# A scan over channel states: GpSimd's products made for two slots at once instead of one

## The chip, the cores and the metric

The kernel runs on one core of a Trainium2 chip. A core has five engines with queues of their own: TensorE (PE in the profile; its weight loads are PEld), VectorE (DVE), ScalarE (ACT), GpSimd (POOL) and SyncE (SP), which here issues all the transfers. Each engine works through its instructions strictly in the order in which the program lists them, and waits at an instruction until semaphores tell that its inputs are there and its output buffer is free. The metric is the device time of one execution in microseconds (us).

## The reference

The input x is 8 samples of 512 channels of 48 x 48 points (2304 points in a row, called L). Two layers are added to it in turn:

```python
x = x + L0_conv_ref(_gn(x), Wq, bq, Wkv, bkv)        # causal linear attention, 8 heads of 64
x = x + L1_conv_ref(_gn(x), in_proj_w, conv_w, ...)  # four blocks of a state-space scan
```

`_gn` is a group norm. The first layer projects to q, k and v, takes elu + 1 of q and k, and sums k v over the points before each point. The second takes the 512 channels as four blocks of 128; a block adds the result of the block before and runs this on its 256 inner channels d and 16 states n:

```python
dA = exp(delta[b,l,d] * A[d,n]);  dBu = delta * xs * Bm[b,l,n]
h = dA_t * h + dBu_t                     # over l, for each d and n
y = sum over n of h * C_t                # then + xs * D, times silu(z), projected to 128
```

so each sample has four blocks one after another, and each block 256 x 16 recurrences of 2304 steps.

## The kernel before, in words

The points are cut into 6 chunks of 384 (`LC`). One chunk of one block of one sample is a *job*; there are 8 x 4 x 6 = 192. A job is cut into 8 *slots* (`SLOTS`): slots 0 to 3 for the first half of the inner channels, 4 to 7 for the second, each slot four recurrences of 128 partitions (two values of `NG`, two groups of channels). The 128 partitions hold 64 channels by two states, so that one job needs 8 x 4 scans. There are 1536 slots and 6144 scans. Two *streams* (samples of even and of odd number) take turns, so that one can prepare while the other scans.

The work of slot k:

- `last_product` (L856, GpSimd): B times delta*xs for the last 128 of the 384 columns (`TAIL`), of both groups and both values of `NG`: 512 elements a partition. It takes the tile `u`, of which there are 5; ScalarE copies the state left by the chunk before into column 0 (L855).
- `product` (L867, VectorE): the same for the first 256 columns, 1024 elements. One input, `dxp`, lies in PSUM, copied there by ScalarE in `inputs` (L840).
- `decay` (L877, ScalarE): exp(delta A) into a PSUM bank, one for each scan, up to three ahead. Six banks are shared with attention's and the preparation's matmuls.
- `scan` (L888, VectorE): four times, over 385 columns in place in `u`.
- `weigh` (GpSimd): copies the last column to `state` (L902, in all but the last chunk) and multiplies `u` by C (L904), 1536 elements a partition.
- `gather` (L911, TensorE): eight matmuls that sum over the states into `yp`. After slots 3 and 7 `gated` (L923, VectorE) multiplies `yp` by silu(z), and `skip` (L845, ScalarE) begins `yp` anew with xs*D.

The order is written out by hand in `slot(k)`: product of slot k+1; in slots 2 and 6 the gated product; tasks that are due (`beside`); the scans; after the second scan the sums of slot k-2, the small product of slot k+2 and again tasks; at the end `weigh` of slot k. A half of a slot is the unit of time in which tasks are due. Tasks are generators that yield at each step the half in which the next one is due, and how many PSUM banks it needs:

- `prepare` of a job, begun 21 halves before its first slot: the convolution and the gate (L693, L704), softplus, delta written to DRAM (`dscr`, L773), then multiplied by xs in place on GpSimd (L805, two products), written again (`xscr`), and all read back spread over the partitions: `dr`, `dxr` (L784) and the rows of B and C (`rows`, L797: for each of four quarters one tile of B and one of C, two transfers of 192 KB each, 4 tiles of each kind).
- `chunk`: attention for one of the four head pairs o and one chunk c; 192 of them, placed by `times` (L293 projects with `wq_sb`, which holds all projections of q, k and v in SBUF, 3 MB). Where o is 0, GpSimd normalises the input first (L317, four pieces).
- `pass_on`: the hand-over from block to block; on GpSimd fu (L662), xi (L667) and xo (L670) for each chunk.
- `statistics` of a sample and `weights` of a block (L539 on GpSimd, four products).

All transfers stand in SP's one queue in the order of these steps; a transfer whose buffer isn't free yet holds up those behind it.

Of the kernel before, what the change touches and what calls it, by code (L numbers as in the profile page):

```python
# [9 lines left out]
F32 = mybir.dt.float32  # L10
# [7 lines left out]
P = 128  # L18
# [32 lines left out]
def attention_then_mamba_kernel(  # L51
# [50 lines left out]
    wq_sb = cpool.tile([P, 4, 1536], F32, name="wq_sb")  # L102
# [3 lines left out]
    def load_projections(o):  # L106

        src = wqkv.rearrange("(t p) c -> p t c", p=P)
        for j in range(3):
            cols = slice(j * 512 + o * P, j * 512 + (o + 1) * P)  # L110
            nc.sync.dma_start(out=wq_sb[:, :, cols], in_=src[:, :, cols])
# [104 lines left out]
    def statistics(b):  # L216
# [3 lines left out]
        if b == 0:  # L220

            xs = []

            def load(c):
                t = mpool.tile([P, 4, 1 + LC], F32, tag="u", name=f"xs_{c}", bufs=5)[:, :, 0:LC]
                nc.sync.dma_start(out=t, in_=xv[:, :, c * LC : (c + 1) * LC])
                xs.append(t)

            for c in range(5):
                load(c)  # L230
            load_projections(0)
            for c in range(NC):
                for ct in range(4):
                    nc.vector.bn_stats(stats[:, ct, c, :], xs[c][:, ct, :])
                if c == 0:
                    load(5)
                    fetch(0)
            for o in range(1, 4):
                load_projections(o)
# [33 lines left out]
    def chunk(m):  # L273
# [16 lines left out]
        def project(j):  # L290
            ps = bank()[:, 0:LC]
            for kt in range(4):
                nc.tensor.matmul(  # L293
                    ps,
                    wq_sb[:, kt, j * 512 + o * P : j * 512 + (o + 1) * P],
# [44 lines left out]
        fetch(m + 1)  # L340
        if o:
# [156 lines left out]
    class Stream:  # L498
# [62 lines left out]
        def pass_on(self):  # L561
# [52 lines left out]
            if last and self.z:  # L614

                got = [
                    mpool.tile([P, 4, 1 + LC], F32, tag="u", name=f"end_{i}", bufs=5)
                    for i in range(NC // 2)
                ]
                for c in range(NC):  # L620
# [53 lines left out]
    class Job:  # L674
# [6 lines left out]
        def prepare(self):  # L681
# [98 lines left out]
            src = scr.rearrange("(q i m f) l -> q m i (f l)", q=4, m=2, i=2)  # L780
# [13 lines left out]
            def rows(m, q):  # L794
                t = mpool.tile([P, NG, LC], F32, tag="BC"[m], name=f"{'BC'[m]}_{n}_{q}", bufs=4)
# [20 lines left out]
            rows(0, 1)  # L816
            self.prepared = True
            yield first - 3, 0
            rows(0, 2)
            yield first - 2, 0  # L820
            rows(1, 0)
            yield first - 1, 0
            rows(0, 3)
            yield first, 0
            rows(1, 1)
# [3 lines left out]
            rows(1, 2)  # L829
            yield first + 3, 0  # L830
            steps(1)
            yield first + 4, 0
            rows(1, 3)

        prepared = closed = False

# [12 lines left out]
        def last_product(self, s):  # L849

            shape, cols = [P, NG, 2, TAIL], slice(LC - TAIL, LC)
            u = mpool.tile([P, NG, 2, 1 + LC], F32, tag="u", name=f"u_{self.n}_{s}", bufs=5)
            if self.c:
                h, q = s // 4, s % 4 * NG
                nc.scalar.copy(u[:, :, :, 0], self.state[:, h, q : q + NG, :])  # L855
# [403 lines left out]
```

## Time and profile before

| what | value |
|---|---|
| runs | 8785.19, 8786.02 and 8791.31 us, median 8786.02 |
| profiled execution, first to last instruction | 8790.1 us, 4.1 over the median |
| first scan, last scan begin at | 229.4 and 8767.3 us |
| busy: VectorE, GpSimd, TensorE, ScalarE | 8067.0, 8044.8, 7766.8, 6744.5 us |
| 6144 scans on VectorE | 5457.0 us, mean 0.939 |
| 1536 products by C on GpSimd | 4882.7 us, mean 3.179 |
| 1536 small products on GpSimd | 1960.9 us, mean 1.277 |
| transfers | 1642.98 MB, 16 engines 69% busy |
| granted TensorE clock, mean | 0.964 |

The profile's own execution spans 8790.1 us; its time on the device is not listed apart from that. "Busy" is the union of an engine's instructions; a product's mean is somewhat longer than the time from its start to the next one's, since neighbours overlap by a few hundredths. A line of the waits says who waited, for whom, the total, how often, and the longest. A line of groups says line, engine, operation, tiles, shapes and count, then the busy time, the mean in ns, and the idle time just before with what ended it. Partitions come first in a shape: 128x1536 is 1536 elements on each of 128 partitions.

### The profile page before, as it was taken

The numbers are of one execution on the slowest core, as the hardware profiler recorded it, in microseconds if no ns is written. First come the engines' busy times: TensorE is split into PE (matmuls) and PEld (weight loads), VectorE is DVE, ScalarE is ACT, GpSimd is POOL, SyncE is SP. The second block draws the span as 40 slices with busy tenths as digits, with TensorE's granted clock in tenths as the row PEclk, the third lists the DMA queues.
The fourth block names the chain that finished last, engine by engine and source line by source line (L and its number), as shares of the span: only waits on it lengthen the run. The fifth ranks groups of instructions, "written<-read, shape, count | busy, mean of one in ns | idle before, by whom it ended". The sixth has DMA issues, their size and how long they took to land.

```text
span 8790.1 us, 122627 instructions
## 1 busy us (share of the span) xinstructions
PE 7766.8 (88%) x36482; PEld 3705.4 (42%) x36482; DVE 8067.0 (92%) x11078; ACT 6744.5 (77%) x13220; POOL 8044.8 (92%) x5623
## 2 busy tenths in 40 slices
PE   7899999998899899998889999999888999999865
PEld 4444444444444444444444444444444444444422
DVE  2899999999899999998889999999889999999998
ACT  2777887777788878777778878877777888877875
POOL 1789999999999999999999999999999999999998
PEclk9999999999999999999999999999999999999977
DMA  5667777766676777776667677777667666766655
GB/s 184 166 174 189 193 197 195 190 188 186 190 191 188 191 195 198 196 190 189 179 190 192 188 191 198 198 195 188 188 183 191 189 187 187 189 187 185 183 156 144
DMA packets 1002907, 1642.98 MB, mean 187 GB/s; under 512 B 138592, under 2 KB 797312, under 8 KB 1002240
## 3 DMA queue, kind: packets, MB, share of 16 engines
q1 hardware_dynamic: 1002240, 1635.13, 69.0%
q8 instruction: 291, 4.77, 0.2%
q14 instruction: 376, 3.08, 0.1%
HBM read 1309.06 MB, written 325.58 MB: 186 GB/s over the span
## 4 chain that ended last, share of the span: by engine, by line
DVE 28%; POOL 20%; ACT 14%; DMA 13%; PE 13%; issue 7%; SPq 4%; POOLq 0%; DVEq 0%; ACTq 0%
DVE u L888 19%; POOL u L904 11%; ACT bank L877 5%; DVE u L867 5%; POOL u L856 4%; PE bank L693 4%; PE bank L293 3%; PE yp L911 3%; DMA C<-scr 3%; SPq L797 2%; DMA dscr<-delta 2%; ACT L877 2%; DMA B<-scr 1%; ACT L764 1%; POOL delta L805 1%
## 5 line engine op out<-in xcount | busy, mean ns | idle before, releaser
L888 DVE TENSOR_TENSOR_SCAN u<-bank,u 128x385 f32<-128x385 f32 (+1 forms) x6144 | 5457.0, 939 | 350.1 <-ACT bank L877 300.3
L904 POOL TENSOR_TENSOR u<-u,C 128x1536 f32<-128x1536 f32 x1536 | 4882.7, 3179 | 121.9 <-DVE gm_m L182 16.9
L877 ACT ACTIVATE bank<-dr,av 128x385 f32<-128x385 f32 (+1 forms) x6144 | 3413.6, 578 | 752.3 <-DVE u L888 611.9
L911 PE MATMUL yp<-u,cst 128*64 128x384 f32 x12288 | 2440.7, 519 | 428.2 <-POOL u L904 355.9
L856 POOL TENSOR_TENSOR u<-B,dxr 128x512 f32<-128x512 f32 x1536 | 1960.9, 1277 | 16.5 <-DMA dxr<-xscr 13.8
L867 DVE TENSOR_TENSOR u<-B,dxp 128x1024 f32<-128x1024 f32 x1536 | 1836.0, 1195 | 11.3 <-ACT dxp L840 11.1
L293 PE MATMUL bank<-xn,wq_sb 128*128 128x384 f32 x4608 | 1680.1, 508 | 82.2 <-POOL xn L317 40.1
L911 PEld LDWEIGHTS yp<-u,cst 128*64 128x64 f32 x12288 | 782.0, 140 | 1660.6 <-issue 842.6
L693 PE MATMUL bank<-xi,wk 128*128 128x384 f32 x3072 | 1117.8, 507 | 218.5 <-ACT kl L390 112.5
L293 PEld LDWEIGHTS bank<-xn,wq_sb 128*128 128x128 f32 x4608 | 849.0, 195 | 826.5 <-DVE u L888 119.6
L693 PEld LDWEIGHTS bank<-xi,wk 128*128 128x128 f32 x3072 | 560.6, 192 | 780.8 <-ACT kl L390 202.1
L805 POOL TENSOR_TENSOR delta<-delta,xs 128x384 f32<-128x384 f32 x384 | 384.4, 1001 | 278.0 <-DMA dscr<-delta 215.9
L305 ACT ACTIVATE ex<-bank,bqkv_sb 128x384 f32<-128x384 f32 x384 | 221.0, 576 | 523.8 <-PE bank L293 523.6
L877 ACT ACT_TABLE_LOAD x382 | 490.1, 1283 | 6.7
L845 ACT ACTIVATE yp<-xs,pv 128x384 f32<-128x384 f32 x384 | 223.8, 583 | 290.8 <-DVE yz L923 289.3
L902 POOL COPY state<-u 128x4 f32<-128x4 f32 x1280 | 242.4, 189 | 172.6 <-DVE u L888 170.0
L753 PE MATMUL bank<-dbc,wd 9*128 9x384 f32 x768 | 315.6, 532 | 1.2 <-ACT dbc L745 1.1
L929 PE MATMUL bank<-yz,wo 128*128 128x384 f32 x768 | 299.2, 506 | 18.5 <-DVE yz L923 14.6
L704 PE MATMUL bank<-xi,wi 128*128 128x384 f32 x768 | 285.9, 494 | 10.9 <-ACT xs L729 10.9
L740 PE MATMUL bank<-xs,wx 128*40 128x384 f32 x768 | 281.0, 489 | 2.6 <-ACT sm L457 2.6
L923 DVE TENSOR_TENSOR yz<-yp,sz 128x384 f32<-128x384 f32 x384 | 211.6, 551 | 62.5 <-PE yp L911 62.3
L423 PE MATMUL bank<-cst,rdb 128*128 128x128 f32 x576 | 113.0, 311 | 170.7 <-DVE u L888 168.5
(117 smaller groups left out, 8018.7 us busy)
## 6 DMA issues: line engine op xcount, KB each, us to landing
B<-scr SPq DMA_DIRECT2D x1536, 192.0 KB
C<-scr SPq DMA_DIRECT2D x1536, 192.0 KB
xn<-xn SPq DMA_DIRECT2D x192, 768.0 KB
dr<-dscr SPq DMA_DIRECT2D x768, 192.0 KB
dxr<-xscr SPq DMA_DIRECT2D x768, 192.0 KB
dscr<-delta SPq DMA_DIRECT2D x192, 384.0 KB
xscr<-delta SPq DMA_DIRECT2D x192, 384.0 KB
xn<-in_x SPq DMA_DIRECT2D x48, 768.0 KB
```

The lines of the kernel that those rows point to most:

```text
L293: nc.tensor.matmul(ps, wq_sb[:, kt, j * 512 + o * P : j * 512 + (o + 1) * P], xn[:, kt, :], start=(kt == 0), stop=(kt == 3),)
L693: nc.tensor.matmul(xc, wk[:, k, h * P : (h + 1) * P], xi[:, c0 + k : c0 + k + LC], start=(k == 0), stop=(k == 3),)
L704: nc.tensor.matmul(zp, wi[:, 256 + h * P : 256 + (h + 1) * P], xi[:, c0 + 3 : c0 + 3 + LC], start=True, stop=True,)
L753: nc.tensor.matmul(vp, wd[32:41, h * P : (h + 1) * P], dbc[32:41, :], start=True, stop=True)
L805: nc.gpsimd.tensor_tensor(delta[:, h, :], delta[:, h, :], xs[:, h, :], ALU.mult)
L856: nc.gpsimd.tensor_tensor(u[:, :, :, 1 + LC - TAIL :], self.B[s % 4][:, :, cols].unsqueeze(2).to_broadcast(shape), self.dxr[s // 4][:, :, ...
L867: nc.vector.tensor_mul(u[:, :, :, 1 : 1 + LC - TAIL], self.B[s % 4][:, :, cols].unsqueeze(2).to_broadcast(shape), self.dxp.unsqueeze(1).to ...
L877: nc.scalar.activation(dA[:, cols], self.dr[h][:, g, cols], AF.Exp, scale=self.w[6][:, 2 * h + g, q + j : q + j + 1],)
L888: nc.vector.tensor_tensor_scan(u[:, j, g, cols], dA[:, cols], u[:, j, g, cols], 0.0, ALU.mult, ALU.add,)
L904: nc.gpsimd.tensor_tensor(h, h, self.C[s % 4].unsqueeze(2).to_broadcast([P, NG, 2, LC]), ALU.mult)
L911: nc.tensor.matmul(self.yp[g * 64 : g * 64 + 64, 0:LC], pair_sum, u[:, j, g, 1:], start=False, stop=(s % 4 == 3 and j == NG - 1), skip_gro ...
L929: nc.tensor.matmul(self.xm[:, 0:LC], self.w[2][:, h, :], self.yz[:, h, :], start=(h == 0), stop=(h == 1),)
```

## The change

One tile `u` now holds two slots, 2p and 2p+1, and there are 3 instead of 5 (six slots instead of five).

- `last_product` makes the small product of both slots in one instruction of 1024 elements, and one state copy on ScalarE. It stands at the start of each odd slot, for the two slots after it, ahead of VectorE's product; before, it stood in the middle of each slot, for the slot two further on.
- `weigh` stands at the end of each odd slot: one copy of the state for both slots and one product by C of 3072 elements. B and C come in two halves instead of four quarters, each in two transfers of 384 KB (2 tiles of each kind); the host orders the rows of the projection for that.
- The scans, VectorE's products and the matmuls stay one slot's each. The sums of slot 2p stand in the middle of slot 2p+3, those of 2p+1 at the start of slot 2p+4; before, those of slot k in the middle of slot k+2.
- The gated product stands after the second scan of slots 2 and 6 instead of ahead of the first; `skip` after the third scan instead of the first.
- The projections' weights no longer lie in SBUF whole: each pass (sample and head pair) loads its own 768 KB in one transfer of contiguous rows, two buffers, issued in the last chunk but one of the pass before.
- At the start all six tiles of x are loaded ahead of the weights; the last hand-over takes its buffers from the larger tiles.

```diff
-            for c in range(5):
+            for c in range(NC):
                 load(c)
-            load_projections(0)
+            load_projections()
...
+        if c == NC - 2:
+            load_projections()
...
-            src = scr.rearrange("(q i m f) l -> q m i (f l)", q=4, m=2, i=2)
+            src = scr.rearrange("(q i m f) l -> q m i (f l)", q=2, m=2, i=2)
...
-            u = mpool.tile([P, NG, 2, 1 + LC], F32, tag="u", name=f"u_{self.n}_{s}", bufs=5)
+            u = mpool.tile([P, 2 * NG, 2, 1 + LC], F32, tag="u", name=f"u_{self.n}_{s}", bufs=3)
...
-                nc.gpsimd.tensor_copy(self.state[:, h, q : q + NG, :], u[:, :, :, LC])
+                nc.gpsimd.tensor_copy(self.state[:, h, q : q + 2 * NG, :], u[:, :, :, LC])
             h = u[:, :, :, 1:]
             nc.gpsimd.tensor_tensor(
-                h, h, self.C[s % 4].unsqueeze(2).to_broadcast([P, NG, 2, LC]), ALU.mult
+                h, h, self.C[s % 4 // 2].unsqueeze(2).to_broadcast([P, 2 * NG, 2, LC]), ALU.mult
             )
...
         end = k + 1 == slots or apart(k + 1)
+        if not end and s % 2 == 1:
+            j, r = at(k + 1)
+            pairs[(k + 1) // 2], (us[k + 1], us[k + 2]) = j.last_product(r)
         if not end and k + 1 not in drawn:
             j, r = at(k + 1)
             j.product(r, us[k + 1])
-        if s == 2 and before is not None and not before.closed:
-            before.gated(1)
-            tasks.insert(0, Task(finale(before)))
-        elif s == 6:
-            job.gated(0)
+        def sums():
+            if waiting and waiting[0][0] <= k - 3:
+                waiting.pop(0)[1]()
+        if s % 2 == 0:
+            sums()
         beside(2 * k)
         for i in range(4):
             job.scan(s, i, us[k], decays.pop(0))
-            if i == 0 and s in (2, 6):
+            if i == 2 and s in (2, 6):
                 job.skip(s // 4)
             ahead(DEPTH)
             if i == 1:
-                if len(waiting) > 1:
-                    waiting.pop(0)()
+                if s % 2 == 1:
+                    sums()
+                if s == 2 and before is not None and not before.closed:
+                    before.gated(1)
+                    tasks.insert(0, Task(finale(before)))
+                elif s == 6:
+                    job.gated(0)
...
-                    us[k + 2] = j.last_product(r)
...
-        u = us[k]
-        job.weigh(s, u)
-        waiting.append(lambda: at(k)[0].gather(s, us.pop(k)))
+        if s % 2 == 1:
+            job.weigh(s - 1, pairs.pop(k // 2))
+            waiting.append((k - 1, lambda: job.gather(s - 1, us.pop(k - 1))))
+            waiting.append((k, lambda: job.gather(s, us.pop(k))))
```

In the changed kernel the small product is L860, the state's copy L906, the product by C L908, the sums L918, VectorE's product L871 and the scans L892.

## The prediction

> **What bounds the kernel now.** I read the page's totals first, then the table by windows, then the waits of all engines, the GpSimd groups by shape, and last the timeline of one undisturbed job.
>
> ```profile
> span 8790.1 us, 122627 instructions
> ...
> PE 7766.8 (88%) x36482; PEld 3705.4 (42%) x36482; DVE 8067.0 (92%) x11078; ACT 6744.5 (77%) x13220; POOL 8044.8 (92%) x5623
> ```
>
> Two engines are level at 92%, and TensorE is close behind. A cut on one alone can't bring more than the other leaves over, so the next question is where each has slack (columns: length, then busy us of PE, PEld, DVE, ACT, POOL, the granted clock, DMA share, GB/s):
>
> ```profile
> 0.00:400.00 400.00, 334.51 (x1697) 182.74 (x1698) 218.00 (x397) 201.00 (x395) 182.55 (x170) 0.96 0.60 176
> 2000.00:2400.00 400.00, 346.76 (x1605) 163.02 (x1605) 359.83 (x493) 300.23 (x583) 376.72 (x281) 0.95 0.70 188
> 4000.00:4400.00 400.00, 344.41 (x1562) 162.23 (x1558) 348.94 (x487) 291.51 (x573) 368.56 (x269) 0.94 0.66 184
> 5200.00:5600.00 400.00, 363.31 (x1747) 175.14 (x1747) 388.84 (x528) 325.77 (x634) 382.67 (x265) 0.99 0.74 198
> 8400.00:8800.00 400.00, 241.98 (x810) 88.41 (x810) 339.37 (x408) 252.11 (x485) 362.88 (x244) 0.78 0.54 146
> ```
>
> In the best window VectorE is busy 388.8 of 400; 11.2 us of idle is the floor that I take. In windows like 2000 and 4000 VectorE falls to 349 to 360 while GpSimd holds 369 to 377: there GpSimd sets the pace. Six windows have VectorE under 373 (those from 2000, 2400, 4000, 4400, 6000 and 6400): VectorE 2177.7 of 2400, GpSimd 2237.0.
>
> ```profile
> ACT ex L305 <- PE bank L293: 523.6, 265, 6.8
> PE yp L911 <- POOL u L904: 355.9, 293, 4.4
> DVE u L888 <- ACT bank L877: 300.3, 212, 4.4
> ...
> POOL delta L805 <- DMA dscr<-delta: 215.9, 93, 25.9
> ...
> DVE u L888 <- POOL u L856: 49.0, 41, 2.9
> ```
>
> VectorE hardly waits for GpSimd directly (49 us). GpSimd's lateness takes a detour: the sums on TensorE wait for L904, everything queued behind them comes late, ScalarE waits for TensorE, and the scans then wait for their decays. If the n-th L904 is set against the end of the fourth scan of the n-th slot, over all 1536, it starts a median 2.6 us late, in a tenth of the slots over 6.2: a backlog.
>
> ```profile
> L904 POOL TENSOR_TENSOR u<-u,C 128x1536 f32<-128x1536 f32 x1536 | 4882.7, 3179 | 121.9 <-DVE gm_m L182 16.9 <-DVE u L888 0.9 <-DMA B<-scr 0.4
> L856 POOL TENSOR_TENSOR u<-B,dxr 128x512 f32<-128x512 f32 x1536 | 1960.9, 1277 | 16.5 <-DMA dxr<-xscr 13.8 <-DMA B<-scr 2.7
> L805 POOL TENSOR_TENSOR delta<-delta,xs 128x384 f32<-128x384 f32 x384 | 384.4, 1001 | 278.0 <-DMA dscr<-delta 215.9 <-ACT bank L877 33.3 <-ACT sm L457 18.8
> L902 POOL COPY state<-u 128x4 f32<-128x4 f32 x1280 | 242.4, 189 | 172.6 <-DVE u L888 170.0 <-DVE gm_a L181 0.5
> ...
> L539 POOL TENSOR_TENSOR wk<-wk,wi 128x256 f32<-128x256 f32 x128 | 93.2, 730 | 7.1 <-DMA wk<-in_wconv 3.6 <-DMA av<-in_alog 3.4
> ```
>
> **GpSimd's fixed cost.** Products of 256, 384 and 512 elements take 730, 1001 and 1277 ns: 2.13 ns an element and 0.184 us that does not depend on size; the copy of 4 elements takes 189 ns, which is nearly that alone. So I price the 3072-element product at 0.184 + 2 x (3.179 - 0.184) = 6.17 us and the 1024-element one at 2 x 1.277 - 0.184 = 2.37. Ends: nothing saved (6.36 and 2.55), or the chord between L856 and L904 (1.857 ns an element, 0.326 fixed: 6.03 and 2.23). Saved: 768 x 2 x 0.184 = 283 us, and 640 state copies of 0.189 = 121 us: 404 of GpSimd's 8045, 5.0% (ends 121 and 621).
>
> The Trainium skill, "GPSIMD Engine Reference", section "3.1 Elementwise", speaks against this: it puts two-input products at about 2.6 cycles an element, measured 4497 ns for 2048 elements. Read as purely by element, a pair would cost 6.75 + 2.25 = 9.0 us against 8.91 now, and only the state copies would be saved. The small shapes' own rows show a fixed part, so I stay with them.
>
> **Where the saving goes.** In the six windows GpSimd sets the pace: 5.0% of 2237.0 is 111 us, within the 155 us that VectorE idles there over the floor (222.3 - 6 x 11.2). Gain 110. In the other fourteen windows from 400 to 8400 VectorE idles 268 us, 112 over the floor, partly for GpSimd (sums late), partly not (transfers, TensorE): I take half, 56; ends 0 and 112.
>
> **New order, possible new stalls.** Now the small product for slot k+2 is issued in the middle of slot k and its scans follow 1.5 slots later. After it, GpSimd does [state 0.27 with its gap, 6.17, odd jobs, 2.37] between the end of a pair's scans and the start of the scans two slots further, against VectorE's 8 scans of 0.888 (5457.0/6144) and three products of 1.195 = 10.7, and about 1.0 of other work (774 us of the rest over 768 pairs). Slots 0,1 of a job: odd job one L805 (0.96), GpSimd 9.8 to 11.7: spare 1.9. Slots 2,3: two products of the block's hand-over (L662, L667), GpSimd 10.7: spare 1.0, least of the four. The best window has this stretch:
>
> ```profile
> 5389.28 1.80 DVE L888 TENSOR_TENSOR_SCAN u<-bank,u 128x385 f32<-128x385 f32 x2
> ...
> 5396.64 3.50 DVE L888 TENSOR_TENSOR_SCAN u<-bank,u 128x385 f32<-128x385 f32 x4
> 5400.06 1.20 DVE L867 TENSOR_TENSOR u<-B,dxp 128x1024 f32<-128x1024 f32 x1
> 5401.17 0.55 DVE L923 TENSOR_TENSOR yz<-yp,sz 128x384 f32<-128x384 f32 x1
> ...
> 5402.10 3.50 DVE L888 TENSOR_TENSOR_SCAN u<-bank,u 128x385 f32<-128x385 f32 x4
> ```
>
> From 5391.1 to 5402.1 it is 11.0 us; the change moves the yz product (0.5) out of it: 10.5 against 10.7, a stall of some 0.2 us in most jobs. Slots 4,5 and 6,7 have no fixed odd job, but GpSimd comes late into the first: 0.27 + 6.17 + 3 x 0.96 + 2.37 = 11.7 against 9.1 (5391.1 to 5400.1), 2.6 behind; 2.6 + 8.8 = 11.4 then stands against 13.7 (to the scans at 5413.84), so it recovers. I charge 0.2 x 150 = 30 us. GpSimd's waits for dscr (215.9 us) stand between the two products now, with 1.9 us to spare; GpSimd reaches L805 about 1 us later than now (6.4 us after the scans instead of 0.27 + 3.14 + 1.24 and a backlog near 1), which takes 93 of the 216 away. Charge 0; ends -49 (the present wait for L856 gone) and +120.
>
> **Edits that I cost at nothing.** *Sums later*: after a pair the product ends 6.4 us behind the scans, the sums stand in mid-slot two slots on, about 7.8: spare 1.4 where it is 4.4 now. TensorE waits more often; its 36.7 us of idle in the best window cover it. Uncovered, the 355.9 us row could double on TensorE. *Three buffers of two slots*: the pair's sums end about one slot before VectorE's next product writes the buffer, and ScalarE's copy of the state waits for the same; about a slot, as now. *B and C in loads of 384 KB*: same bytes, 1536 fewer issues on SP of some 0.6 us; C's second load waits on SP for GpSimd's last product of the job before, some 1.2 us and its lag, with steps(1) and attention's fetches queued behind; they are due a slot or more later. *wq* loaded anew for each of 32 passes: 25.2 MB instead of 3.1, 4 us of transfer each at 198 GB/s, beside 0.7 of DMA share; bare it would cost 128 us. *skip* after the third scan: follows the yz product as before. 640 copies fewer on ScalarE (0.19 each) are off the path.
>
> **Ends.** At the start SP spends 6.6 and 10.5 us issuing the 12 strided loads of wq, the sixth x tile behind the first three; one contiguous load stands in their place: -10 (0 to -17). At the end the last product is a pair's: 3.0 + 1.5 us more, +5.
>
> **Sum.** -110 - 56 + 30 - 10 + 5 = -141 from a span of 8790.1, which lies 4 us over the runs' median of 8786.0: 8649 in the profile, 8645 in the runs.
>
> **Rivals.**
> A, VectorE's floor everywhere: all 267 us over the floor go, no new stall, start as above: 8786 - 267 - 5 = 8514. For it: GpSimd is the root of the detour. Against: waits for transfers and TensorE (91% busy in the best window) remain.
> B, hidden: the windows at 349 us are held by transfers and attention's normalisation (xn, L317), not by GpSimd's throughput, or GpSimd's cost is purely by element. Then half of the 56 and the 10 at the start are gained, and 30 + 5 given back: 8783.
> C, slower: the short loop. Each pair's small product stands behind the pair before's large one, with 1 to 2 us to spare instead of more than a slot. GpSimd's waits for others (215.9 + 64.7 + 33.3 + 20.5 + 18.8 = 353 us), 49 of which reach the scans today, then reach them whole: +304, with half of the gain (-83) and the rest: 8786 + 304 - 83 + 25 = about 9030; at half that, 8880. It decides once the added waits pass 141 us, 0.18 us a pair.
>
> **Chances.** Forecast 0.46 (8570 to 8740), A 0.12, B 0.14, C 0.28. A measurement tells 0.2%, 18 us, from no change. Faster: 0.46 + 0.12 + 0.04 of B = 0.62. Same: 0.07 of B and 0.01 of C's mild edge = 0.08. Slower: 0.27 of C and 0.03 of B = 0.30. The range runs from A's 8510 to C at half strength, 8880, leaving out half of A's tail and half of C.
>
> **What would show it.** In the profile after: L908 at 6.0 to 6.4 us x768 and L860 near 2.4; GpSimd's busy time near 7640 and VectorE's still 8067; the windows from 2000 and 4000 at over 365 on VectorE; the scans' wait for the small product (L860) under 100 us in all, TensorE's wait for L908 under 500. I am wrong if L908 takes twice 3.18, if the scans' wait for L860 passes 200 us, or if sums wait so much that ScalarE's wait for TensorE (523.6) grows.

## The result and the profile after

The changed kernel takes 9450.91 us (median of 4 runs, 9440.34 to 9452.48) where the kernel before took 8788.67 beside it: 1.0743 times as long, 95% interval 1.073 to 1.0757. The forecast was 8645 with a range up to 8880; it was wrong in sign and by 806 us. The profiled execution spans 9438.5 us.

The totals of the page after:

```profile
span 9438.5 us, 115980 instructions
...
PE 8050.1 (85%) x36482; PEld 3774.4 (40%) x36482; DVE 8243.5 (87%) x11078; ACT 6705.7 (71%) x12580; POOL 7740.4 (82%) x3447
```

GpSimd is busy 304 us less, as meant, and idles 1698 us instead of 745. VectorE is busy 176 us *more* with the same 11078 instructions. No engine is over 87% any more: what bounds the kernel is not one engine but a chain between them. The mean granted clock of TensorE fell from 0.964 to 0.928. The chain that ended last says the same (share of the span by engine):

```profile
POOL 28%; PE 22%; DVE 20%; ACT 12%; issue 9%; DMA 8%; SPq 2%; POOLq 0%; ACTq 0%; DVEq 0%
```

Before it was VectorE 28%, GpSimd 20%, TensorE 13%. The windows of 400 us (columns as before: PE, PEld, DVE, ACT, POOL, clock, DMA share, GB/s):

```profile
2000.00:2400.00 400.00, 345.30 (x1542) 161.36 (x1543) 350.59 (x486) 288.80 (x544) 353.95 (x176) 0.91 0.69 187
4000.00:4400.00 400.00, 346.52 (x1560) 162.16 (x1559) 363.18 (x498) 284.61 (x537) 339.08 (x153) 0.93 0.68 178
5200.00:5600.00 400.00, 343.63 (x1578) 161.21 (x1577) 356.06 (x474) 288.85 (x546) 326.25 (x138) 0.94 0.65 173
8400.00:8800.00 400.00, 344.74 (x1571) 161.69 (x1568) 354.85 (x474) 288.13 (x537) 328.39 (x143) 0.93 0.64 169
```

The window from 5200, the best one before with VectorE at 388.8, is now like the rest: 356. GpSimd, which held 369 to 377 in the weak windows, is at 326 to 354. The loss is spread evenly, which points to something that every job does. The waits name it (who waited for whom: total us, times, longest):

```profile
ACT bank L881 <- DVE u L892: 1267.2, 1614, 5.8
...
POOL state L906 <- DVE u L892: 734.0, 313, 14.1
ACT ex L308 <- PE bank L296: 730.4, 381, 6.8
PE yp L918 <- POOL u L908: 678.3, 265, 8.0
DVE yz L930 <- PE yp L918: 607.9, 338, 11.7
POOL delta L813 <- DMA dscr<-delta: 303.8, 84, 24.1
...
DVE u L892 <- ACT bank L881: 211.1, 210, 6.8
...
DVE u L892 <- POOL u L860: 176.2, 162, 3.5
```

and the groups by shape (the last two numbers ahead of the second bar are busy us and mean ns):

```profile
L908 POOL TENSOR_TENSOR u<-u,C 128x3072 f32<-128x3072 f32 x768 | 4736.1, 6167 | 159.3 <-DVE gm_m L185 81.4 <-issue 11.8 <-DVE u L892 6.3
L860 POOL TENSOR_TENSOR u<-B,dxr 128x1024 f32<-128x1024 f32 x768 | 1816.4, 2365 | 41.8 <-PE yp L918 17.5 <-DMA dxr<-xscr 17.2 <-DMA B<-scr 3.6
...
L930 DVE TENSOR_TENSOR yz<-yp,sz 128x384 f32<-128x384 f32 x384 | 213.0, 555 | 608.1 <-PE yp L918 607.9
L588 DVE TENSOR_SCALAR wt<-wt 128x2 f32<-128x2 f32 x32 | 144.5, 4515 | 0.3 <-ACT wt L586 0.3
```

In the kernel before, the gated product's wait and the addition that is L588 here read:

```profile
DVE yz L923 <- PE yp L911: 62.3, 39, 6.6
```

```profile
L583 DVE TENSOR_SCALAR wt<-wt 128x2 f32<-128x2 f32 x32 | 16.6, 519 | 0.3 <-ACT wt L581 0.3
```

Three things are to be seen. VectorE's gated product (`yz`, L930) waits 607.9 us for the sums on TensorE, where it waited 62.3 before. TensorE's sums wait 678.3 us for the product by C, where it was 355.9. GpSimd waits 734.0 us for the scans, where it was 170.0: its backlog is gone, and it stands idle because VectorE comes late. And one small thing: L588, an addition of 1 to two numbers a partition, takes 4515 ns instead of 519 (it was L583 before), 32 times.

VectorE's own account closes: the span grew by 648.4 us = 176.5 of busy time (127.9 of it L588) + 471.9 of idle. In the idle, `yz` is +546, the scans' wait for the small product L860 +127 (49.0 to 176.2), their wait for the decays -89 (300.3 to 211.1), and `q` (L355) waiting for ScalarE -75 (102.4 to 27.2). Counted by slot of a job (each from its first scan to the next slot's), VectorE's idle goes from 85 to 525 us in slot 2, where the gated product closes the job before (523 of it is `yz`), and from 7 to 204 in slot 6, where the other gated product now stands; slot 5, at whose end that one stood before, falls from 104 to 35, and slot 7 from 287 to 130.

### One job's close, in the trace

GpSimd, TensorE and VectorE of the kernel after at the end of one job (start, length, instruction, and in brackets the idle time just before and who ended it):

```profile
5036.39 0.19 POOL L906 COPY state<-u 128x8 f32<-128x8 f32 x1 [3.33 <-DVE u L892]
5036.66 6.15 POOL L908 TENSOR_TENSOR u<-u,C 128x3072 f32<-128x3072 f32 x1
```

```profile
5038.11 1.55 PE L761 MATMUL bank<-dbc,wd 9*128 9x384 f32 x4
5042.87 2.83 PE L918 MATMUL yp<-u,cst 128*64 128x384 f32 x8 [3.20 <-POOL u L908]
5045.62 0.83 PE L428 MATMUL bank<-cst,rdb 128*128 128x128 f32 x3
5046.30 2.75 PE L296 MATMUL bank<-xn,wq 128*128 128x384 f32 x8
5048.97 1.51 PE L918 MATMUL yp<-u,cst 128*64 128x384 f32 x8
```

```profile
5045.12 1.20 DVE L871 TENSOR_TENSOR u<-B,dxp 128x1024 f32<-128x1024 f32 x1
5046.23 1.80 DVE L892 TENSOR_TENSOR_SCAN u<-bank,u 128x384 f32<-128x384 f32 x2
5050.53 0.56 DVE L930 TENSOR_TENSOR yz<-yp,sz 128x384 f32<-128x384 f32 x1 [2.50 <-PE yp L918]
```

The scans of slot 7 end at 5036.3. The product by C for slots 6 and 7 ends at 5042.8. TensorE has come to the sums of slot 6 by 5039.7, stands 3.20 us, and does them in 2.83 us where the next eight, of the same form, take 1.51. Then it does 3.4 us of attention (L428, L296) that stands between the two slots' sums, and the sums of slot 7. Meanwhile VectorE has done slots 0 and 1 of the next job and half of slot 2, and reaches the gated product at 5048.0: 2.5 us too early.

Over jobs 4 to 189 (means of my own count from the two traces): before, the product by C of slot 7 ended 4.35 us behind the scans and its sums were done 3.77 us before the gated product was due. After, it ends 6.47 behind; TensorE has stood 2.57 before the sums of slot 6, does them in 2.60 instead of 1.46, has 4.13 us of attention behind them, then the sums of slot 7, and the gated product follows 0.06 later, having waited 2.69.

### The profile page after: what moved, and what is told of

It reads as the page before. It is cut to its first block, busy times and chain, and to the rows that moved or that the text cites. A ratio compares the mean times of both kernels' runs of the same rounds, so it can differ in the third digit from the quotient of the medians.

```text
span 9438.5 us, 115980 instructions
## 1 busy us (share of the span) xinstructions
PE 8050.1 (85%) x36482; PEld 3774.4 (40%) x36482; DVE 8243.5 (87%) x11078; ACT 6705.7 (71%) x12580; POOL 7740.4 (82%) x3447
## 4 chain that ended last, share of the span: by engine, by line
POOL 28%; PE 22%; DVE 20%; ACT 12%; issue 9%; DMA 8%; SPq 2%; POOLq 0%; ACTq 0%; DVEq 0%
POOL u L908 19%; DVE u L892 12%; PE yp L918 8%; PE bank L296 6%; POOL u L860 4%; DMA dscr<-delta 4%; DVE u L871 3%; ACT bank L881 3%; PE bank L701 2%; ACT L881 2%; ACT L737 2%; POOL delta L813 2%; PE bank L712 1%; DVE wt L588 1%; POOL fu L670 1%
## 5 line engine op out<-in xcount | busy, mean ns | idle before, releaser
L892 DVE TENSOR_TENSOR_SCAN u<-bank,u 128x385 f32<-128x385 f32 (+1 forms) x6144 | 5477.1, 940 | 389.8 <-ACT bank L881 211.1
L908 POOL TENSOR_TENSOR u<-u,C 128x3072 f32<-128x3072 f32 x768 | 4736.1, 6167 | 159.3 <-DVE gm_m L185 81.4
L918 PE MATMUL yp<-u,cst 128*64 128x384 f32 x12288 | 2570.0, 544 | 692.1 <-POOL u L908 678.3
L860 POOL TENSOR_TENSOR u<-B,dxr 128x1024 f32<-128x1024 f32 x768 | 1816.4, 2365 | 41.8 <-PE yp L918 17.5
L871 DVE TENSOR_TENSOR u<-B,dxp 128x1024 f32<-128x1024 f32 x1536 | 1835.6, 1195 | 5.3 <-ACT dxp L844 5.2
L296 PE MATMUL bank<-xn,wq 128*128 128x384 f32 x4608 | 1724.3, 521 | 7.5 <-ACT delta L772 3.9
L918 PEld LDWEIGHTS yp<-u,cst 128*64 128x64 f32 x12288 | 809.3, 146 | 2026.5 <-issue 1064.4
L296 PEld LDWEIGHTS bank<-xn,wq 128*128 128x128 f32 x4608 | 916.5, 207 | 690.3 <-issue 108.8
L813 POOL TENSOR_TENSOR delta<-delta,xs 128x384 f32<-128x384 f32 x384 | 383.8, 1004 | 576.5 <-DMA dscr<-delta 303.8
L930 DVE TENSOR_TENSOR yz<-yp,sz 128x384 f32<-128x384 f32 x384 | 213.0, 555 | 608.1 <-PE yp L918 607.9
L308 ACT ACTIVATE ex<-bank,bqkv_sb 128x384 f32<-128x384 f32 x384 | 223.2, 581 | 730.4 <-PE bank L296 730.4
L906 POOL COPY state<-u 128x8 f32<-128x8 f32 x640 | 124.6, 195 | 749.2 <-DVE u L892 734.0
L712 PE MATMUL bank<-xi,wi 128*128 128x384 f32 x768 | 330.8, 512 | 106.0 <-ACT xs L737 106.0
L467 PE MATMUL bank<-xr,cst 128*128 128x384 f32 x384 | 192.0, 584 | 160.3 <-DVE u L892 156.0
L481 PE MATMUL bank<-sm,v 128*64 128x128 f32 x2304 | 269.2, 314 | 0.0
```

The costliest lines, as they stand in the source:

```text
L296: nc.tensor.matmul(ps, wqs[m // NC][:, kt, j * P : (j + 1) * P], xn[:, kt, :], start=(kt == 0), stop=(kt == 3),)
L712: nc.tensor.matmul(zp, wi[:, 256 + h * P : 256 + (h + 1) * P], xi[:, c0 + 3 : c0 + 3 + LC], start=True, stop=True,)
L813: nc.gpsimd.tensor_tensor(delta[:, h, :], delta[:, h, :], xs[:, h, :], ALU.mult)
L860: nc.gpsimd.tensor_tensor(u[:, :, :, 1 + LC - TAIL :], self.B[s % 4 // 2][:, :, cols].unsqueeze(2).to_broadcast(shape), self.dxr[s // 4][: ...
L871: nc.vector.tensor_mul(u[:, :, :, 1 : 1 + LC - TAIL], self.part(self.B, s)[:, :, cols].unsqueeze(2).to_broadcast(shape), self.dxp.unsqueez ...
L892: nc.vector.tensor_tensor_scan(u[:, j, g, cols], dA[:, cols], u[:, j, g, cols], 0.0, ALU.mult, ALU.add,)
```

## The experiments

All ratios are against the kernel before, with 95% intervals. The suspects at first were four: the product for two slots (its lateness makes the sums late), the small product's short loop, the new order of sums, gated product and `skip`, and the transfers.

### First set: which part of the change costs?

**e1: the product by C slot by slot.** From the kernel after; `job.weigh` at the end of every slot, on its half of the tile.

```diff
+        job.weigh(s, us[k])
         if s % 2 == 1:
-            job.weigh(s - 1, pairs.pop(k // 2))
+            pairs.pop(k // 2)
```

> The changed kernel with GpSimd's product by C and its copy of the state made slot by slot again (1536 elements, 1536 times), at the end of each slot; tiles, small products, transfers and places of the sums stay as changed. Theory 1 (the double product comes 3 us later, TensorE stands before the sums of slots 6 and 7, and the gated product of slot 2 waits for them): VectorE's wait for the gated product falls from 608 us to under 150, time 8800 to 8950. Theory 2 (tiles, transfers or the short way from the double product to the next small product): the time stays over 9250.

Measured: 9590.75 us, 1.0904 (1.0888 to 1.092). Slower still, so theory 1 in the form put here fell. It is no clean undo, though. Two rows of its waits:

```profile
DVE u L892 <- POOL u L860: 579.2, 402, 5.2
...
DVE yz L930 <- PE yp L918: 283.4, 135, 5.2
```

The wait of `yz` halves, but the small product, left at the start of the odd slot, now stands in GpSimd's queue behind the even slot's product, and the scans wait for it 579 us. This is rival C's mechanism; it exists, but in the kernel after it had only 176 us. How much the place matters shows against h2 below, which differs from e1 in nothing but that it issues the small product in the middle of the even slot: 9062.81 us against 9590.75. With the small product at the start of the odd slot, the double product by C is even the faster one, 9450.91 against 9590.75.

**e2: the gated product half a slot later.** From the kernel after; `gated(1)` and `skip(0)` ahead of the scans of slot 3.

```diff
+        if s == 3:
+            if before is not None and not before.closed:
+                before.gated(1)
+                tasks.insert(0, Task(finale(before)))
+            job.skip(0)
...
```

> The changed kernel with the gated product of the job before (and skip of the new one) half a slot later, ahead of slot 3's scans instead of in the middle of slot 2. Theory 1: the gated product's wait falls by 300 to 450 of its 523 us, time 9000 to 9200. Theory 2: the wait only moves to another place, time within 60 us of 9440.

Measured: 9681.07 us, 1.1005 (1.0988 to 1.1021). The wait of `yz` falls to 148.2 and the time grows by another 230:

```profile
DVE rd L411 <- PE bank L408: 270.7, 64, 14.2
DVE q L355 <- ACT bank L309: 261.1, 156, 6.0
```

The time lies outside what either theory expected. More time for the sums doesn't help: what stands behind comes late instead.

**e4: the order alone.** From the kernel before, single slots everywhere; the sums a half slot later, the gated product after the second scan, `skip` after the third.

```diff
...
+        if len(waiting) > 2:
+            waiting.pop(0)()
...
-            if i == 0 and s in (2, 6):
+            if i == 2 and s in (2, 6):
...
-                if len(waiting) > 1:
-                    waiting.pop(0)()
+                if s == 2 and before is not None and not before.closed:
+                    before.gated(1)
...
```

> The kernel before with the changed order alone: sums of a slot half a slot later (start of slot k+3), the gated product after the second scan, skip after the third; all products slot by slot, five tiles. Theory 1: the order costs little where the product is single, 8740 to 8880. Rival: the late order itself makes the gated product wait, over 9100.

Measured: 9203.41 us, 1.0463 (1.0442 to 1.0484), `yz` waiting 431.0. The order costs 4.6% with no pairing at all, and not by the gated product alone: the sums also free the tile `u`, and later sums free it later. VectorE's product, which had next to no such wait before, has this row:

```profile
DVE u L867 <- PE yp L911: 181.5, 156, 1.9
```

**e5 and f3: the transfers.** e5 is the kernel before with weights loaded anew in each pass and B and C in halves; f3 has the halves alone.

```diff
+        if c == NC - 2:
+            load_projections()
...
-            src = scr.rearrange("(q i m f) l -> q m i (f l)", q=4, m=2, i=2)
+            src = scr.rearrange("(q i m f) l -> q m i (f l)", q=2, m=2, i=2)
...
```

> The kernel before with the changed transfers alone: the projections' weights loaded anew for each pass, B and C in halves of 384 KB. Theory 1: within 20 us of the kernel before. Theory 2 (transfers): over 9000.

> The kernel before with B and C in halves of 384 KB alone; the projections' weights stay resident. If the weights' loads cost the 60 us seen with both edits: 8780 to 8805. If the halves do: 8835 to 8865.

Measured: e5 8857.04 us, 1.0071 (1.0056 to 1.0086); f3 8807.14, 1.0017 (1.0008 to 1.0026). Both edits that I costed at nothing cost something: the halves some 12 us, the weights' reload some 50.

### Second set: the sums, and the held addition

**f1: both slots' sums together**, in the middle of the odd slot, a half slot ahead of where the second ones were.

```diff
-        if s % 2 == 0:
-            sums()
...
-                if s % 2 == 1:
-                    sums()
+                while waiting and s % 2 == 1:
+                    waiting.pop(0)[1]()
```

> The changed kernel with the sums of slot 2p+1 moved half a slot earlier, directly behind those of slot 2p in the middle of slot 2p+3, ahead of the tasks there; all else as changed. Theory 1, as it now stands (between the sums of slot 6 and those of slot 7 TensorE does a half slot of attention's matmuls, 4.1 us, and that makes the gated product late): VectorE's wait for the gated product falls from 608 us to under 150, time 9000 to 9200. Rival (the double product alone makes the sums late, wherever they stand): wait over 400, time over 9350.

Measured: 9388.85 us, 1.0675 (1.0659 to 1.0691), some 60 less than after. `yz` hardly waits now (30.6), yet most of its 600 us is paid elsewhere:

```profile
PE yp L918 <- POOL u L908: 619.2, 233, 7.8
DVE q L355 <- ACT bank L309: 414.4, 188, 6.0
...
DVE u L892 <- POOL u L860: 166.7, 145, 3.4
```

TensorE still stands in front of the sums, attention's matmuls behind them come late, and VectorE's next step of attention takes over the wait.

**f2 and f4: the addition on ScalarE**, from the kernel after and from f1.

```diff
                 nc.scalar.activation(wt[:, 0:2], wt[:, 2:4], AF.Exp, scale=-1.0 / L)
+                nc.scalar.activation(wt[:, 0:2], wt[:, 0:2], AF.Copy, bias=1.0)
                 yield "1", 0
-                nc.vector.tensor_scalar_add(wt[:, 0:2], wt[:, 0:2], 1.0)
```

> The changed kernel with the addition of 1 in the hand-over (two elements a partition, 32 times, 4.5 us each on VectorE, ending 0.02 to 0.03 us after a GpSimd product) made on ScalarE instead. If VectorE is held there until GpSimd's running product ends, and that is on the path: 100 to 140 us less, 9310 to 9350, VectorE's busy time down by about 145. Rival (held, but beside other waits): within 40 us of 9447.

> f1_sums_together and f2_add_on_scalar in one. If the held addition and the rest add up: 130 to 170 under f1's 9389, so 9220 to 9260; what is then left over k4_together_single is the price of the double product's lateness alone.

Measured: f2 9294.55 us, 1.0572 (1.0554 to 1.0589); f4 9207.02, 1.0473 (1.0459 to 1.0488). That is some 150 less than the kernel after and 182 less than f1 (130 to 170 were expected), for 32 instructions on two elements a partition. Why they are slow stands in the timeline of the kernel after:

```profile
1197.55 1.20 DVE L871 TENSOR_TENSOR u<-B,dxp 128x1024 f32<-128x1024 f32 x1
1198.66 5.48 DVE L588 TENSOR_SCALAR wt<-wt 128x2 f32<-128x2 f32 x1
1204.18 0.17 DVE L589 RECIPROCAL wt<-wt 128x2 f32<-128x2 f32 x1
```

```profile
1197.97 6.15 POOL L908 TENSOR_TENSOR u<-u,C 128x3072 f32<-128x3072 f32 x1
```

The addition ends at 1204.14, 0.02 us behind GpSimd's product (1197.97 + 6.15 = 1204.12); 31 of the 32 end 0.02 to 0.03 us behind a GpSimd product. It is held until the running product is done, and VectorE's whole queue with it. It was held before too, 24 times of 32, but mostly for some 0.2 us, as it came when GpSimd's product was nearly done (519 ns mean).

**k2: the same edit in the kernel before.**

> The kernel before with the hand-over's addition on ScalarE alone. The addition takes 0.52 us on VectorE there, 0.35 of it held: 0 to 20 us less than before. More than 50 less would say that the addition costs by more than its hold.

Measured: 8769.79 us, 0.9977 (0.9967 to 0.9987): 22 us faster, for 16.6 us of VectorE's time.

### Third set: from before to after step by step

**g1: the small product paired**, in before's order (middle of the even slot), with after's tiles and transfers; product by C, sums and gated product as before.

```diff
-                    us[k + 2] = j.last_product(r)
+                    if r % 2 == 0:
+                        _, (us[k + 2], us[k + 3]) = j.last_product(r)
```

> The kernel before with the small product alone made for two slots (three tiles of two slots, in the middle of each even slot, ahead of the products by C as before), with the transfers of the changed kernel; products by C, state copies, sums and gated product as before. If only the order and the double product by C cost: 0 to 100 us under the 8857 of the transfers alone. Rival (three double tiles, or the small product's doubled length): over 8900.

Measured: 8821.43 us, 1.0028 (1.0017 to 1.0039); 36 less than e5. None of it comes from the start (all of x is loaded ahead of the weights here): the first scan begins at 226.3 us, in e5 at 222.3. Pairing the small product helps.

**h2: g1 with after's places** for sums, gated product and `skip`; the product by C still single.

```diff
-                if len(waiting) > 1:
-                    waiting.pop(0)()
+                if s % 2 == 1:
+                    sums()
+                if s == 2 and before is not None and not before.closed:
+                    before.gated(1)
...
```

> The kernel with the small product alone for two slots (8821 us), given the changed kernel's places of the sums, the gated product and skip; the product by C and the state's copy stay single. What it has over 8821 is the price of the places, what is left to 9447 that of the double product by C with the small product behind it. Theory 1: 9150 to 9300, so some 400 and 200. Rival (the places cost only with the double product): under 8950.

Measured: 9062.81 us, 1.0301 (1.0287 to 1.0315), so the places cost 242, between what the two theories expected. Some 50 of it is the held addition (2232 ns against 658 in g1, 32 times). The product by C of slot 7 ends 3.64 us behind the scans here, and TensorE doesn't stand before slot 6's sums at all; yet slot 7's sums begin 6.55 us after those are done, and the gated product waits 1.78 us a job (means over jobs 4 to 189, counted as above). So it is the place of slot 7's sums that makes the gated product wait, and it does so without a double product. The sums also free the tiles, for which GpSimd's small product waits here and not in g1. The two rows:

```profile
DVE yz L927 <- PE yp L915: 557.1, 296, 6.5
...
POOL u L860 <- PE yp L915: 171.8, 119, 4.5
```

**k4: h2 with f1's places**, so f1 with the product by C single.

```diff
...
-                if s % 2 == 1:
-                    sums()
+                while s % 2 == 1 and waiting and waiting[0][0] <= k - 2:
+                    waiting.pop(0)[1]()
```

> f1's places (both slots' sums in the middle of slot 2p+3) with the product by C single, small product for two slots, everything else as in h2_late_single. If f1's 9389 us come from the double product itself (TensorE stands 2.3 us before the sums and comes out at a low clock, VectorE's held addition): 8820 to 8950 here. If they come from the places: over 9100.

Measured: 8907.7 us, 1.0132 (1.0118 to 1.0146). This and f1 are the closest pair of the study: the same places of sums, gated product and `skip`, and product by C with state copies for one slot here and for two there. They differ in one thing more: the small product is issued in the middle of the even slot here, at the start of the odd slot in f1. Single is 481 us faster. TensorE's wait for the product is down from 619.2 us to 85.6, the scans' wait for the small product from 166.7 to 28.8, and the wait of `q` from 414.4 to near the 102.4 of the kernel before:

```profile
DVE q L355 <- ACT bank L309: 127.9, 74, 6.0
...
PE yp L915 <- POOL u L908: 85.6, 55, 5.1
```

Part of the 481 is the held addition: 4298 ns against 2225 here, 66 us of VectorE's time at the least, and no more than the 182 that taking it away from f1 was worth. The other 300 to 415 belong to the double product and what it makes late; up to 138 of them can be the small product, which comes late to the scans and stands elsewhere in f1.

**j1: the sums early, the gated product in mid-slot**, from h2.

```diff
...
                 job.skip(s // 4)
+                waiting.pop(0)[1]()
...
+                if len(waiting) > 1 and s not in (2, 6):
+                    waiting.pop(0)[1]()
```

> h2_late_single with the sums back in the middle of slot k+2, but for those of slots 0 and 4, which follow skip behind the third scan; the gated product stays in mid-slot. If what the places cost (242 us) is the sums standing late, behind half a slot of other matmuls, ahead of the gated product: 8800 to 8880, the gated product's wait under 100. If it is the gated product's place: over 8980.

Measured: 9090.28 us, 1.034 (1.0325 to 1.0354). `yz` waits 4.9 us only, and yet it isn't faster than h2; the scans wait 572.0 us for their decays on ScalarE (366.7 in g1). So late sums alone are not the price of the places: with early ones j1 pays as much, and k4's order pays far less than both.

**h1 and h5: both slots' sums at the start of slot 2p+4**, so the first ones half a slot later than in the kernel after, the gated products ahead of slots 3 and 7; h5 with the addition on ScalarE besides.

```diff
         if s % 2 == 0:
-            sums()
+            while waiting and waiting[0][0] <= k - 3:
+                waiting.pop(0)[1]()
+        if s == 3:
+            if before is not None and not before.closed:
+                before.gated(1)
...
```

> The changed kernel with both slots' sums at the start of slot 2p+4, and the gated product (with skip behind it) ahead of the scans of slots 3 and 7. Theory 1 in its present form (TensorE stands 2.6 us a job at the sums of slot 6 until the double product is done, comes out with a low clock, and what stands behind it on TensorE, sums or projections, is late for VectorE): the sums find the product done, TensorE's wait for L908 falls from 678 us to under 150, time 8950 to 9200. Rival (the short way from the double product to the next small product, or the buffers' later release, sets the pace): over 9350.

> h1_sums_at_start with the hand-over's addition on ScalarE. The addition gave 150 us in the changed kernel: the same again, 120 to 180 under h1. Less than 60 would say that the hold overlapped with what h1 removes.

Measured: h1 9880.61 us, 1.1236 (1.122 to 1.1251), the slowest of all; h5 9767.62, 1.1108 (1.1093 to 1.1123), 113 less and short of the 120 to 180 expected. Here TensorE hardly stands in front of the sums (72.6 us) and `yz` hardly waits (11.5). The theory that the stand on TensorE is the price fell with this; the time is on the rival's side. Among its waits:

```profile
POOL state L906 <- DVE u L892: 1089.4, 335, 14.6
...
PE bank L428 <- DVE u L892: 472.9, 150, 3.9
...
DVE u L892 <- ACT bank L881: 436.2, 245, 8.6
...
PE bank L701 <- POOL xi L675: 362.2, 92, 11.6
DVE u L892 <- POOL u L860: 323.9, 175, 5.0
```

The lateness stands in other places; the rival's short way from the double product to the small one is one of them (323.9 us, 176.2 in the kernel after), but not the largest.

**g2: the better version.** g1 with each pass's weights in four loads of 192 KB over four chunks, and the addition on ScalarE.

```diff
-        if c == NC - 2:
-            load_projections()
+        if 1 <= c <= 4 and (len(wqs) < 4 * B or m < (4 * B - 1) * NC):
+            load_projections(c - 1)
```

> The kernel with the small product alone for two slots, the weights' 768 KB in four loads of 192 KB spread over a pass, and the hand-over's addition on ScalarE. If the 50 us of the weights came from one long transfer ahead of others, and VectorE's hold costs 10: 8760 to 8800, level with the kernel before or 0.4% faster. If the added bytes themselves cost: 8805 to 8825.

Measured: 8766.43 us, 0.9965 (0.9952 to 0.9979): the only version with a pair in it that beats the kernel before, by 0.35%. It is level with k2, which has the addition's edit alone; the paired small product pays for the transfers that it needs and no more.

### What the steps add up to

| from | to | edit | us |
|---|---|---|---|
| before 8795 | f3 8807 | B and C in halves | +12 |
| f3 | e5 8857 | weights loaded anew in each pass | +50 |
| e5 | g1 8821 | small product for two slots, start | -36 |
| g1 | h2 9063 | places of sums, gated product, `skip` | +242 |
| h2 | after, some 9451 | product by C and state copy for two slots, small product at the start of the odd slot | +388 |

The held addition has a share in the last two rows: its time on VectorE is 21.0 us in g1, 71.4 in h2 and 144.5 in the kernel after, so some 50 and at least 73 us. The last row is two edits in one. Taken by way of e1, moving the small product alone costs 528 us and pairing the product by C then gives 140 back; by way of f1 and k4, where the sums stand together, the two edits cost 481. What the double product costs is thus not one number: it depends on where the small product and the sums stand.

## Why the prediction was wrong

**GpSimd's fixed cost: right.** 6.17 and 2.37 us were forecast, 6.167 and 2.365 came. The state copy of 8 elements takes 195 ns against 189 for 4. The Trainium skill's figure ("GPSIMD Engine Reference", "3.1 Elementwise"), read as purely by element, gives 6.75 as an estimate; that reading doesn't hold here.

**GpSimd busy near 7640: 7740.** The groups' own sums fell by 409 us (4882.7 to 4736.1, 1960.9 to 1816.4, 242.4 to 124.6 for the state copies), as forecast at 404; the union of its instructions fell by 304. The difference over 2176 fewer instructions is 0.048 us each, the stretch by which neighbours overlap: a quarter of what I priced as fixed cost was never time on the queue.

**"Gain 110" in the windows where GpSimd sets the pace, and 56 elsewhere: did not come.** GpSimd got 304 us, and the windows from 2000 and 4000 went to 350.6 and 363.2 on VectorE instead of over 365. More room on GpSimd didn't bring them there. My reading is that the pace there is set not by GpSimd's throughput alone but by the loop scans, product by C, sums, gated product, which the pairing makes longer while it makes the engine freer.

**"Sums later", costed at nothing: the step that failed.** I set the product's end (6.4 us behind the scans, measured 6.47) against the time of the middle of slot 2p+3 (7.8, in the job shown 7.2) and read 1.4 us of spare; TensorE's idle was to cover the rest. The product's arrival was right. What was not asked is what must be done by the middle of slot 2, when VectorE's gated product is due. That is not the product but, behind it, slot 6's sums (2.60), attention's matmuls (4.13) and slot 7's sums (1.56): 8.3 us on TensorE, where VectorE leaves some 5.6 (8.3 less the 2.69 that the gated product waits). Before, slot 6's sums stood a slot earlier and had their product then. The runs put the price on the order first: alone it costs some 240 us (h2) and 410 (e4), with products for one slot that are there in time. In h2 TensorE doesn't stand before slot 6's sums, and the gated product waits 557.1 us all the same, for slot 7's sums behind half a slot of attention. The product for two slots adds to that a common late end for both slots' sums. The bound that I gave, "the 355.9 us row could double on TensorE", came nearly true (678.3), but I took TensorE's idle to be all that it would eat; VectorE lost as well: 546 us of `yz`. Of my own marks for being wrong, the third was hit: ScalarE's wait for TensorE (523.6) grew to 730.4.

**Not foreseen at all: the held addition**, 128 us on VectorE directly, some 150 in the time. The row that could have warned was in the trace of before (L583, shown above): 519 ns for two elements, where the reciprocal of the same two takes 166.

**"Edits that I cost at nothing", the transfers: wrong by 62 us,** 50 of it the weights, inside the bare 128 that was named for them. "Beside 0.7 of DMA share" was no cover for one load of 768 KB. Of the 55 us between g1 and g2 some 22 is the addition (k2), which leaves some 33 of the 50 to the loads in four parts.

**The short loop: mis-sized.** 30 us were charged; the scans' wait for L860 rose by 127 to 176.2, just short of the 141 of added waits at which rival C was to decide and of the 200 in all that was named as a mark. C ended on the right side, but its mechanism is a part of the loss at most; e1 and h2 show that it can be far dearer. GpSimd's wait for `dscr`, of which 93 us were to go, grew from 215.9 to 303.8. B's half that GpSimd's cost is purely by element is refuted by L908's own row.

**The start: right.** -10 was forecast; the first scan starts at 221.2 us instead of 229.4.

**What stays open.** That the double product, with the small product behind it, costs 300 to 415 us beyond the held addition is shown by k4 against f1; how much of that is late sums and how much the late small product (up to 138) isn't separated. Three tries to hide the lateness by moving its users failed: e2, f1 and h1 each took one wait away and got others. Why the places alone cost 242 (h2) or 269 (j1) and only 86 in k4's order isn't settled. My reading, argued only from the orders: in h2 the last sums stand half a slot ahead of the gated product that needs them, in j1 the next sums stand directly behind the `skip` that needs the gated product, and k4 alone has a whole slot on either side. It isn't enough: g1 has less than k4 on either side and pays nothing, and TensorE's wait for `skip` is no longer in j1 (61.7 us) than in g1 (72.2). The tiles' later release is another candidate for h2, where GpSimd's small product waits 171.8 us for it, but not for j1, where that wait is 1.4. Of k4's 86, some 50 is the addition (2225 against 658 ns, 32 times). What the low clock costs by itself was not tried.

## What to carry to other kernels

An engine at 92% isn't a bound to be relieved by larger instructions if its result goes round a loop of in-order queues: the saved fixed cost (304 us here) is throughput, the doubled instruction (3.18 to 6.17 us) is latency, and here a lateness of a few microseconds a job cost more. When sums or any other step are moved, find the instruction that is due last in the loop (here VectorE's gated product), and add up all that its producer's queue does between the late input and it, not only the late input's arrival. Look for small instructions with a mean far above that of their neighbours of the same size: each may be a hold-up that longer instructions elsewhere lengthen.

## What the runs showed of the hardware

**A small VectorE instruction waits out GpSimd's.** An addition on 128x2 from SBUF to SBUF takes 5.48 us beside a product of 6.15 and ends 0.02 us after it; an addition of two SBUF tensors of 128x4 (L193, eight times) went from a mean of 929 ns to 2424, as two of the eight were held for a whole product before and three after. Not every small one is held: the reciprocal of 128x2 behind it takes 0.17 while GpSimd's next product already runs. The Trainium skill has the rule ("SBUF — State Buffer", "SBUF: two separate sides"): a GpSimd instruction and a VectorE one that has two SBUF inputs or runs in a mode with two ports contend for a port pair, and whichever starts first has it for the whole instruction, while the other is blocked. The trace agrees for the two additions: up to GpSimd's longest instruction is the price of each.

**TensorE is slow after a stand.** The granted clock in three stretches of 4 us around the close shown (same columns as the windows above):

```profile
5038.00:5042.00 4.00, 1.67 (x6) 0.66 (x4) 3.90 (x10) 2.94 (x6) 4.00 (x1) 1.00 0.41 80
5042.00:5046.00 4.00, 3.13 (x10) 1.15 (x11) 4.00 (x5) 3.96 (x7) 3.78 (x4) 0.61 0.44 120
5046.00:5050.00 4.00, 4.00 (x19) 2.11 (x17) 2.03 (x3) 1.37 (x3) 4.00 (x1) 0.97 1.01 212
```

In the stretch in which the 3.20 us without work end it is granted 0.61, and eight sums take 2.83 us instead of 1.51: a wait of 3.2 us costs TensorE 4.5.

**One load of 768 KB is not four of 192 KB.** Reloading the weights cost some 50 us in one transfer of contiguous rows (e5 against f3); in four, spread over four chunks, some 33 of that came back (g1 to g2, less k2's 22; by difference, not tried alone).
